# Making the first panel's neighbour masks earlier in a two-layer graph-attention kernel

## The chip, the cores and the metric

The kernel runs on one core of a Trainium2 chip. The metric is the device time of one execution in microseconds (us). A core has five engines with instruction streams of their own: TensorE (PE, matmuls), VectorE (DVE), ScalarE (ACT), GpSimd (POOL) and SyncE (SP). Here SP issues the loads and POOL the stores. Data lies in HBM, in the on-chip SBUF, and in eight PSUM banks that PE writes.

## The reference

Two attention layers over a graph of N = 2708 nodes with D = 1024 features, in float32:

```
h = relu(layernorm(x))
f, g = h @ Wf + bf, h @ Wg + bg
e = relu(f @ g.T)
x = x + softmax(where(adj > 0, e, -9e15)) @ (h @ W + bW)        # layer 0

h2 = relu(layernorm(x)) @ W1
e = leaky_relu(h2 @ a1 + (h2 @ a2).T, 0.2)
x = x + relu(softmax(where(adj > 0, e, -9e15)) @ h2)            # layer 1
```

`adj` is a 2708 x 2708 matrix of int32 zeros and ones. What the change touches is the mask made of it, in layer 0's first panel.

## The kernel before, in words

**Tiling.** The scores are made transposed, and their columns are cut into five panels of 512 to 576 (`NP = 5`). The rows run in ten pairs of 128-row tiles (`NQ = 10`); what is left over makes an eleventh unit, `LEFT`. Each product of 2 x 2 blocks is made with seven multiplications, `M1` to `M7` (Strassen's scheme).

**Stages of the beginning.** f @ g.T is h @ (Wf Wg^T) @ h.T plus bias terms, so the kernel first makes M = Wf Wg^T: a loop over `a` = 0 to 7 makes the first half rows (L607 to L624, `half_row_of_M(a, 0)`, tile M_ps), and a second loop the other half rows (L625 to L630). Meanwhile the x rows are loaded, normalized, transposed by PE (h_ps, hsT) and, for each pair, stored with their block sums in HBM (`hs_d`, and `hg_d` for the aggregation). Then `project_q(0)` (L686) multiplies M with the first panel's h (tiles qx to qz), and `scores(0)` (L1360) makes the first panel's scores pair by pair: seven products, their left sides As loaded from `hs_d`, the results in the banks sx, sy, sz. Then the next panel's projection begins (qx again), and the maximum of the scores, `acc`, is transposed by PE into mx_ps.

**Masks.** `mask_maker(p)` (L769) gives three functions for a panel. `fetch(q)` loads a pair's adjacency: four loads of adj_i (128 KB each) into a buffer of the stream pool and four of adj_t into a slot; for LEFT twice as many. `convert(q)` makes 0 or -BIG of it (nm, two DVE instructions). `turn(q, k)` transposes it in blocks of 32 x 32 (mask, two DVE instructions), and after k = 1 stores the mask in HBM (mk_d) for the second layer. In `scores` a mask is added, with a relu, by `finish`.

Before, the first masks were made beside `project_q(0)`: the hooks of its product M1 fetch pairs 0 and 1, that of M2 converts pair 0, that of M7 turns it (`first_masks`, L830). In `scores`, pair q fetches q + 2 before its first product (L1414), converts q + 1 after M5 (L1432), and turns it after M2 and M7 (L1437, L1442).

**What sets the order.** Loads go out in program order from one queue, `load` (L137), so a load that waits for its buffer holds up all behind it. Buffers come from pools in turn: 54 slots of 2304 bytes a partition, 12 stream buffers of 4 KB, 8 PSUM banks. A load's buffer is free once its last reader is through; in the scores some of the stream buffers hold rows (hsT) that a store to `hs_d` is still reading.

Work that isn't on the way of the matmuls (x rows, sums, stores) lies in a list `later`. `behind(us)` (L214) grants the list a budget of DVE time after each product, and takes items from it while the budget lasts. Each item can have a fetch, which is issued up to five items (`ahead`) before its turn. Among them are the sums of rows of `hg_d` (`sums_h`, L365; tile hr: loaded by SP, added on DVE, stored by POOL) that follow the x rows. The items' order in the list is fixed; where each falls between the products follows from these budgets, and the scheduler that builds the program may move DVE instructions that aren't held to program order.

Of the kernel before, what the change touches and what calls it, by code (L numbers as in the profile page):

```python
# [25 lines left out]
M1, M5, M6, M7, M3, M2, M4 = range(7)  # L26
# [31 lines left out]
def kernel(  # L58
# [19 lines left out]
    nc = InOrder(tc)  # L78
# [6 lines left out]
    NP = N // W  # L85
# [3 lines left out]
    width = [W + NM, W + NM, W + NY, W, W]  # L89
    base = [sum(width[:p]) for p in range(NP)]  # L90
    F = W // P
# [4 lines left out]
    start_of_tile = lambda t: base[t // F] + t % F * B32  # L96
# [40 lines left out]
    def load(o, i):  # L137
        for a, b in in_16(o, i):
            tc.keep_in_program_order(nc.sync.dma_start(a, b))

    def store(o, i):
        for a, b in in_16(o, i):
            nc.gpsimd.dma_start(a, b)  # L143
# [29 lines left out]
    mk_d = [dram.tile([P, NQ + 1, 2, width[p]], BF, name=f"mk_d{p}") for p in range(NP)]  # L173
# [7 lines left out]
    minus_half, minus_big = (consts.tile([P, 1], FP, name=f"minus{i}") for i in range(2))  # L181
# [243 lines left out]
    c0 = consts.tile([P, 1], FP, name="c0")  # L425
# [157 lines left out]
    def left_of_q(k):  # L583
# [9 lines left out]
        side_of_q(M7, k, a21)  # L593
        side_of_q(M4, k, a22)

    first_h = both("hT")
    make_pairs()
    ws = fetch_wg(0)
# [8 lines left out]
    for a in range(NC):  # L607
        for i in range(2 * a, min(2 * a + 2, NC)):
            if i + 2 < NC:
                rows_of_wf[i + 2] = load_rows(wf, i + 2, "wf")  # L610
            transposed_wf(i)
        half_row_of_M(a, 0)
        if a == NH:
            dot(c0, halves(bfb), halves(bgb))
            vb = [slot(f"vb{g}") for g in range(2)]
            for g in range(2):
                spread(vb[g][:, :W], [v[:, 4 * g + j:4 * g + j + 1] for j in range(4)])
            ws = fetch_wg(1)
        bias_of_g(a, ws)
        if a == NH + 2:  # L620
            transposed_wg(1, ws)
        behind(2.0 if a < NH else 5.0, True)
        if a == 1:
            nc.hold = ()  # L624
    for k in range(NH):  # L625
        for a in (k, k + NH):
            half_row_of_M(a, 1)
            wfT.pop(a)
            behind(5.5, True)
        left_of_q(k)  # L630
# [6 lines left out]
    for name, gs in (("pick_lo", (0, 1)), ("pick_hi", (0, 2, 3))):  # L637
        t = consts.tile([P, P], FP, name=name)
# [124 lines left out]
                   rate=1.2 if p == 0 else 1.5, room=(M1, M2, M7, M4) if p == 0 else ())  # L763
        return B


    mk_sb = {}

    def mask_maker(p):  # L769

        r0, w = base[p], width[p]
        NG, NB = P // B32, W // B32
        tail = -(-(w - W) // B32)
        raw, neg = {}, {}

        def columns(q):

            if q < LEFT:
                return [[start_of_tile(t) + P * g for g in range(NG)] for t in pairs[q]]
            return [[base[g // 2] + W + g % 2 * B32 for g in range(NG)], [base[2] + W] * NG]  # L780

        def fetch(q):
            a = stream("adj_i", (P, NB, 2, B32), I32)
            b = slot("adj_t", (P, tail, 2, B32), I32) if tail else None
            raw[q] = a, b
            c0, c1 = columns(q)

            def square_rows(t, blocks, g, k, r, j, n):
                load(t[B32 * g:B32 * (g + 1), :, k] if k is not None else
                     t[B32 * g:B32 * (g + 1)].rearrange("p b k c -> p b (k c)"),  # L790
                     adj[r:r + blocks * B32, j:j + n].rearrange("(b r) j -> r b j", r=B32))
            for t, blocks, r in ((a, NB, r0), (b, tail, r0 + W)):
                for g in range(NG if t is not None else 0):
                    if q < LEFT:
                        square_rows(t, blocks, g, None, r, c0[g], 2 * B32)
                    else:
                        for k, c in enumerate((c0, c1)):
                            square_rows(t, blocks, g, k, r, c[g], B32)

        def convert(q, by_act=False):  # L800
            a, b = raw.pop(q)
            neg[q] = []
            for t, blocks in ((a, NB), (b, tail)):
                if t is not None:
                    m = slot("nm", (P, 2, blocks, B32), BF)
                    if by_act and t is a:
                        nc.scalar.activation(m, t.rearrange("p b k c -> p k b c"), AF.Sign, bias=minus_half)
                        nc.scalar.activation(m, m, AF.Identity, bias=minus_big, scale=BIG / 2)
                    else:
                        nc.vector.tensor_scalar(m, t.rearrange("p b k c -> p k b c"), 0.0, -BIG, op0=OP.is_le, op1=OP.mult)  # L810
                    neg[q].append(m)

        def turn(q, k):
            if k == 0:
                mk_sb[p, q] = slot("mask", (P, 2, WX), BF)
            mk = mk_sb[p, q]
            m = neg[q]
            nc.vector.transpose(mk[:, k, :W].rearrange("p (s g r) -> p g s r", s=F, g=NG),
                                m[0][:, k].rearrange("p (g s) c -> p g s c", g=NG))
            if tail:  # L820
                nc.vector.transpose(mk[:, k, W:W + tail * B32].rearrange("p (b r) -> p b r", r=B32), m[1][:, k])
            if k == 1:
                neg.pop(q)
                store(mk_d[p][:, q], mk[:, :, :w])

        return fetch, convert, turn

    makers = [mask_maker(p) for p in range(NP)]

    def first_masks(p, step):  # L830
        fetch, convert, turn = makers[p]
        if step == 0:
            fetch(0)
            fetch(1)
        elif step == 1:
            convert(0)
        else:
            turn(0, 0)
            turn(0, 1)

    def load_mask(p, q, k):
        mt = slot("maskl", (P, WX), BF)
# [517 lines left out]
    def scores(p, B):  # L1360

        w = width[p]
        h = w // 2
        lo, hi = slice(0, h), slice(h, w)
        fetch, convert, turn = makers[p]
# [5 lines left out]
        acc = slot("acc")  # L1371
        S = [None] * NT
        rates = (0.6, 1.0, 0.65, 0.65, 0.65)
        lefts = {}

        def product(q, m, ps, start):
# [33 lines left out]
        for q in range(NQ):  # L1410
            n = P
            make_until(q + 2)
            rate = 1.3 if NQ - 1 not in made else rates[p]
            if q + 2 <= LEFT:  # L1414
                fetch(q + 2)
            if p in ORDERED and q in (2, 6):
                (copy_residual if q == 2 else bias_residual)(p)
            sa, sb = slot("Sa"), slot("Sb")
            S[pairs[q][0]], S[pairs[q][1]] = sa, sb
            X, Y, Z = (bank(f"s{k}") for k in "xyz")  # L1420
            m1, t = slot("sm1"), slot("st")
            product(q, M1, X, True)
            for s in (lo, hi):
                add(m1[:n, s], X[:n, :h], rb[:n, s])
            if left_over:
                left_over()
            product(q, M6, Z, True)
            add(t[:n, lo], Z[:n, :h], m1[:n, hi])
            behind(rate, True)
            product(q, M5, Y, True)  # L1430
            add(t[:n, hi], Y[:n, :h], m1[:n, hi])
            if q + 1 <= LEFT:  # L1432
                convert(q + 1, p > 0)
# [21 lines left out]
        t = stream("As", (P, 2, NH, P))  # L1455
# [245 lines left out]
    def take_softmax(p):  # L1701
        got["sm"] = softmax(p, got["S"], got["m"])

    B = project_q(0, {M1: lambda: first_masks(0, 0), M2: lambda: first_masks(0, 1), M7: lambda: first_masks(0, 2)})
    G = {}
    for p in range(NP):
        got["S"], got["acc"] = scores(p, B)
# [7 lines left out]
        if p + 1 < NP:  # L1715
            B = project_q(p + 1, hooks)
# [157 lines left out]
```

## Time and profile before

| | us |
|---|---|
| median of 3 runs | 3078.0 (3077.63 to 3078.73) |
| the profiled execution | 3082.24 |
| its span, first to last instruction | 3080.5 |
| PE busy | 3000.0 (97%) |
| DVE busy | 2046.6 (66%) |
| ACT busy | 551.7 (18%) |
| POOL busy | 505.5 (16%) |

The stages that the change touches, by the profiled execution:

| from, to (us) | stage | PE busy | DVE busy | share of the DMA engines |
|---|---|---|---|---|
| 0 to 70 | loads, first half rows of M | 58.84 of 70 | 34.76 | 0.68 |
| 70 to 157 | half rows of M, second part | 85.36 of 87 | 69.23 | 0.94 |
| 157 to 181 | projection of panel 0 begins | 24.00 of 24 | 15.16 | 0.98 |
| 181 to 224 | projection, first scores | 43.00 of 43 | 29.82 | 0.76 |
| 224 to 400 | scores of panel 0, next projection begins | 158.06 of 176 | 119.97 | 0.92 |
| 400 to 3080.5 | the rest, four panels and layer 1 | 2630.72 of 2680.5 | 1777.69 | 0.75 |

How to read it: a busy time is the union of an engine's instructions without those that only wait or issue a DMA. A row of a timeline gives start, length, engine, line of the kernel, operation, output and inputs by tile name, shape, count, and in square brackets the idle time just before it and what ended it ("<-DMA As<-hs_d": the landing of a load of As). L45 and L139 are helpers through which all DVE instructions and all loads go, so these are told apart by their tiles. PE at full clock needs 2.1 us for one product of eight matmuls on 288 columns.

### The profile page before, as it was taken

What the parts mean: (1) busy time and instruction counts of PE and PEld (TensorE: products, weight loads), DVE (VectorE), ACT (ScalarE), POOL (GpSimd) and SP (SyncE); (2) the same over time, 40 slices, a digit from 0 to 9 for tenths busy, and PEclk for the clock granted to TensorE, in tenths of its full rate; (3) what the DMA queues carried; (4) which work ended last, traced back from release to release, by engine and by line L of the source; (5) the groups of instructions that cost most, each with busy time, mean ns of one, the idle gap of its engine ahead of it and who ended that gap; (6) DMA issues with size and microseconds to landing.
All of it is one profiled execution on the core that took longest, in us unless ns stands there. A gap on an engine that the chain in (4) does not pass through costs nothing.

```text
span 3080.5 us, 41669 instructions
## 1 busy us (share of the span) xinstructions
PE 3000.0 (97%) x14630; PEld 2301.1 (75%) x14630; DVE 2046.6 (66%) x4577; ACT 551.7 (18%) x895; POOL 505.5 (16%) x786
## 2 busy tenths in 40 slices
PE   8998999899999999999999999998999999999998
PEld 4576777657877588885888886784767959879695
DVE  5776693776661586715965276867878768787853
ACT  3420020021110121101211011302222131212200
POOL 1421101310011110214102011131202010020202
PEclk9999999999999999999999999998999999999999
DMA  6988967987565786758967588679757768878786
GB/s 220 304 259 245 302 248 251 314 285 228 177 241 146 226 262 218 247 155 240 284 206 253 165 233 275 230 292 323 250 193 266 260 203 295 289 268 297 266 293 249
DMA packets 447809, 766.80 MB, mean 249 GB/s; under 512 B 175488, under 2 KB 262304, under 8 KB 447568
## 3 DMA queue, kind: packets, MB, share of 16 engines
q1 hardware_dynamic: 392624, 598.30, 60.1%
q0 software_dynamic: 54976, 165.83, 16.1%
q8 instruction: 116, 1.90, 0.2%
q14 instruction: 93, 0.76, 0.1%
HBM read 630.04 MB, written 138.11 MB: 249 GB/s over the span
## 4 chain that ended last, share of the span: by engine, by line
PE 79%; DVE 9%; DMA 5%; issue 5%; SPq 1%; ACT 1%; POOL 0%; POOLq 0%; DVEq 0%; ACTq 0%
PE sz L1385 7%; PE gz L664 6%; PE gx L664 6%; PE gy L664 6%; PE gz L1074 5%; PE pz L1274 5%; PE sx L1385 5%; PE px L1274 4%; PE sy L1385 4%; PE py L1274 4%; PE gx L1074 3%; PE gy L1074 3%; PE gv L664 3%; PE M_ps L577 3%; PE qz L664 3%
## 5 line engine op out<-in xcount | busy, mean ns | idle before, releaser
L1385 PE MATMUL sz<-B,As 128*128 128x288 f32 (+2 forms) x1200 | 292.7, 393 | 3.4 <-DVE st L45 3.3
L1385 PEld LDWEIGHTS sz<-B,As 128*128 128x128 f32 x1200 | 228.1, 191 | 53.0 <-DVE st L45 6.8
L1385 PE MATMUL sx<-B,As 128*128 128x288 f32 (+2 forms) x800 | 203.0, 397 | 13.5 <-DMA As<-hs_d 12.0
L1385 PE MATMUL sy<-B,As 128*128 128x288 f32 (+2 forms) x800 | 199.0, 392 | 0.0
L664 PE MATMUL gz<-Sa,hc 128*128 128x288 f32 (+2 forms) x800 | 190.3, 399 | 6.3 <-DMA hc<-hg_d 6.3
L1385 PEld LDWEIGHTS sx<-B,As 128*128 128x128 f32 x800 | 153.4, 192 | 47.5 <-DMA As<-hs_d 8.0
L664 PEld LDWEIGHTS gz<-Sa,hc 128*128 128x128 f32 x800 | 154.5, 194 | 40.4 <-DMA hc<-hg_d 6.7
L1385 PEld LDWEIGHTS sy<-B,As 128*128 128x128 f32 x800 | 151.7, 190 | 30.6 <-DVE st L45 0.3
L1074 PE MATMUL gz<-quarter,hc 128*128 128x128 f32 (+2 forms) x1344 | 168.8, 279 | 3.8 <-DVE gT L45 3.7
L143 POOL DMA_DIRECT2D out_dram<-x_res x180 | 89.1, 501 | 482.0 <-DVE x_res L45 473.5
L1074 PEld LDWEIGHTS gz<-quarter,hc 128*128 128x128 f32 x1344 | 160.6, 191 | 5.1 <-DVE gT L45 4.6
L1274 PE MATMUL px<-w,gT 128*128 128x512 f32 x320 | 141.2, 593 | 1.5 <-ACT pt L45 1.5
L1274 PE MATMUL py<-w,ps 128*128 128x512 f32 x320 | 142.2, 593 | 0.0
L1274 PE MATMUL pz<-w,ps 128*128 128x512 f32 x320 | 142.1, 594 | 0.0
L143 POOL DMA_DIRECT2D mk_d<-mask x55 | 36.0, 654 | 523.7 <-DVE mask L45 517.3
L1274 PEld LDWEIGHTS pz<-w,ps 128*128 128x128 f32 x320 | 60.2, 190 | 76.2 <-issue 70.5
L1274 PEld LDWEIGHTS py<-w,ps 128*128 128x128 f32 x320 | 60.5, 190 | 75.1 <-issue 72.7
L1274 PEld LDWEIGHTS px<-w,gT 128*128 128x128 f32 x320 | 60.1, 190 | 72.9 <-issue 67.1
L577 PE MATMUL M_ps<-wgT,wfT 128*128 128x512 f32 x256 | 112.5, 595 | 1.6 <-ACT hsT L45 1.6
L664 PE MATMUL gy<-T,hc 128*128 128x288 f32 (+2 forms) x480 | 111.6, 394 | 0.0
L45 ACT ACTIVATE P<-P 128x576 f32<-128x576 f32 (+2 forms) x110 | 72.0, 655 | 207.5 <-DVE P L45 207.4
L984 POOL TENSOR_TENSOR gT<-gT,rr 128x2304 f32<-128x2304 f32 (+5 forms) x12 | 44.4, 3700 | 378.0 <-DVE rr L45 172.7
(382 smaller groups left out, 5892.1 us busy)
## 6 DMA issues: line engine op xcount, KB each, us to landing
hc<-hg_d SPq DMA_DIRECT2D x175, 512.0 KB
As<-hs_d SPq DMA_DIRECT2D x150, 512.0 KB
hc<-hr_d SPq DMA_DIRECT2D x119, 512.0 KB
hc<-hs_d SPq DMA_DIRECT2D x112, 512.0 KB
w<-wt_d SPq DMA_DIRECT2D x96, 512.0 KB
w<-in_L_gnn_W_dram SPq DMA_DIRECT2D x72, 512.0 KB
md<-md_d SPq DMA_DIRECT2D x56, 512.0 KB
adj_i<-in_adj_dram SPq DMA_DIRECT2D x200, 128.0 KB
```

The lines of the kernel that those rows point to most:

```text
L45: i = f(*a, **k)
L143: nc.gpsimd.dma_start(a, b)
L577: nc.tensor.matmul(ps, wfT[a][c // NH][:, c % NH, :], wgT[b][c], start=(c == 0), stop=(c == NC - 1))
L664: nc.tensor.matmul(ps[d], left(m, k, d), right(m, k), start=(start and k == 0), stop=(k == K - 1), skip_group_check=True)
L984: nc.gpsimd.tensor_tensor(of(e, s), of(e, s), by(s, k), OP.mult)
L1074: nc.tensor.matmul(ps[:, d], lhs[:, d * P:(d + 1) * P], inner_right(m, n, k), start=(start and k == 0 and d == 0), stop=(k == NK - 1), ski ...
L1274: nc.tensor.matmul(ps, left[i][m][:, k, :], w_[k], start=(start and k == 0), stop=(k == NH - 1), skip_group_check=True)
L1385: nc.tensor.matmul(ps[:n, :h], lefts[q][:, i % 2, c, :n], B[m][c // 2][:, c % 2, :h], start=(start and c == 0), stop=(c == NH - 1), skip_g ...
```

## The change

The mask code moves up, ahead of the M stage, as it is. A new function `early_masks(q, step)` does one of three steps for a pair of panel 0. In the loop of M's first half rows, pair 0 is fetched at a = 2, converted at a = 3 and turned at a = 4; pair 1 at a = 4, 5 and 6. The hooks of `project_q(0)` now only fetch pair 2. In the scores of panel 0, `more` is 1, so that fetch, convert and turns each run one pair further ahead than before; in the other panels nothing is changed. The calls for the other panels keep `first_masks`.

```diff
+    def early_masks(q, step):
+        fetch, convert, turn = makers[0]
+        if step == 0:
+            fetch(q)
+        elif step == 1:
+            convert(q)
+        else:
+            turn(q, 0)
+            turn(q, 1)
...
         behind(2.0 if a < NH else 5.0, True)
         if a == 1:
             nc.hold = ()
+        for m in range(2):
+            if 2 <= a - 2 * m <= 4:
+                early_masks(m, a - 2 * m - 2)
...
         rates = (0.6, 1.0, 0.65, 0.65, 0.65)
+        more = int(p == 0)
...
-            if q + 2 <= LEFT:
-                fetch(q + 2)
+            if q + 2 + more <= LEFT:
+                fetch(q + 2 + more)
...
-            if q + 1 <= LEFT:
-                convert(q + 1, p > 0)
+            if q + 1 + more <= LEFT:
+                convert(q + 1 + more, p > 0)
...
-            if q + 1 <= LEFT:
-                turn(q + 1, 0)
+            if q + 1 + more <= LEFT:
+                turn(q + 1 + more, 0)
...
-            if q + 1 <= LEFT:
-                turn(q + 1, 1)
+            if q + 1 + more <= LEFT:
+                turn(q + 1 + more, 1)
...
-    B = project_q(0, {M1: lambda: first_masks(0, 0), M2: lambda: first_masks(0, 1), M7: lambda: first_masks(0, 2)})
+    B = project_q(0, {M1: lambda: early_masks(2, 0)})
```

More of the change, by code (lines that the diff above doesn't have):

```diff
@@ L594, in left_of_q, with mask_maker, columns, fetch @@
         side_of_q(M4, k, a22)
+    mk_sb = {}
+    def mask_maker(p):
+        r0, w = base[p], width[p]
+        NG, NB = P // B32, W // B32
+        tail = -(-(w - W) // B32)
+        raw, neg = {}, {}
+        def columns(q):
+            if q < LEFT:
+                return [[start_of_tile(t) + P * g for g in range(NG)] for t in pairs[q]]
+            return [[base[g // 2] + W + g % 2 * B32 for g in range(NG)], [base[2] + W] * NG]
+        def fetch(q):
+            a = stream("adj_i", (P, NB, 2, B32), I32)
+            b = slot("adj_t", (P, tail, 2, B32), I32) if tail else None
+            raw[q] = a, b
+            c0, c1 = columns(q)
+            def square_rows(t, blocks, g, k, r, j, n):
+                load(t[B32 * g:B32 * (g + 1), :, k] if k is not None else
+                     t[B32 * g:B32 * (g + 1)].rearrange("p b k c -> p b (k c)"),
+                     adj[r:r + blocks * B32, j:j + n].rearrange("(b r) j -> r b j", r=B32))
+            for t, blocks, r in ((a, NB, r0), (b, tail, r0 + W)):
+                for g in range(NG if t is not None else 0):
+                    if q < LEFT:
+                        square_rows(t, blocks, g, None, r, c0[g], 2 * B32)
+                    else:
+                        for k, c in enumerate((c0, c1)):
+                            square_rows(t, blocks, g, k, r, c[g], B32)
+        def convert(q, by_act=False):
+            a, b = raw.pop(q)
+            neg[q] = []
+            for t, blocks in ((a, NB), (b, tail)):
+                if t is not None:
+                    m = slot("nm", (P, 2, blocks, B32), BF)
+                    if by_act and t is a:
+                        nc.scalar.activation(m, t.rearrange("p b k c -> p k b c"), AF.Sign, bias=minus_half)
+                        nc.scalar.activation(m, m, AF.Identity, bias=minus_big, scale=BIG / 2)
+                    else:
+                        nc.vector.tensor_scalar(m, t.rearrange("p b k c -> p k b c"), 0.0, -BIG, op0=OP.is_le, op1=OP.mult)
+                    neg[q].append(m)
+        def turn(q, k):
+            if k == 0:
+                mk_sb[p, q] = slot("mask", (P, 2, WX), BF)
+            mk = mk_sb[p, q]
+            m = neg[q]
+            nc.vector.transpose(mk[:, k, :W].rearrange("p (s g r) -> p g s r", s=F, g=NG),
+                                m[0][:, k].rearrange("p (g s) c -> p g s c", g=NG))
+            if tail:
+                nc.vector.transpose(mk[:, k, W:W + tail * B32].rearrange("p (b r) -> p b r", r=B32), m[1][:, k])
+            if k == 1:
+                neg.pop(q)
+                store(mk_d[p][:, q], mk[:, :, :w])
+        return fetch, convert, turn
@@ new lines, with first_masks @@
+    makers = [mask_maker(p) for p in range(NP)]
+    def first_masks(p, step):
+        fetch, convert, turn = makers[p]
+        if step == 0:
+            fetch(0)
+            fetch(1)
+        elif step == 1:
+            convert(0)
+        else:
+            turn(0, 0)
+            turn(0, 1)
+    def early_masks(q, step):
+        fetch, convert, turn = makers[0]
+        if step == 0:
+            fetch(q)
+        elif step == 1:
+            convert(q)
+        else:
+            turn(q, 0)
+            turn(q, 1)
@@ L764, in project_q @@
         return B
[L767 to L839, printed above, removed]
     def load_mask(p, q, k):
```

## The prediction

> **What bounds the kernel now.** I read the page's busy times first, then the waits of TensorE (PE) in the stretch that the change touches, then the timeline of each wait.
>
> ```profile
> PE 3000.0 (97%) x14630; PEld 2301.1 (75%) x14630; DVE 2046.6 (66%) x4577; ACT 551.7 (18%) x895; POOL 505.5 (16%) x786
> ```
>
> PE is busy 3000.0 of 3080.5 us. The change adds, drops and reorders no PE instruction (in the built programs PE's order is the same), so it can only shorten or lengthen what PE idles. PE's waits from 45 us to 400 us (engine and line, what it waited for, sum, times, longest):
>
> ```profile
> PE sx L1385 <- DMA As<-hs_d: 12.0, 3, 7.5
> PE mx_ps L856 <- DVE acc L45: 5.9, 1, 5.9
> PE M_ps L577 <- ACT hsT L45: 1.6, 1, 1.6
> ```
>
> That is 19.5 us in five places. The timeline gives the places (start, length, work, idle ahead of it and its releaser), and the granted clock in three stretches says what follows a wait (the columns after the busy times are clock, DMA share, GB/s):
>
> ```profile
> 74.09 6.28 PE L577 MATMUL M_ps<-wgT,wfT 128*128 128x512 f32 x14 [1.64 <-ACT hsT L45]
> ...
> 249.34 4.21 PE L1385 MATMUL sx<-B,As 128*128 128x288 f32 x8 [7.52 <-DMA As<-hs_d]
> ...
> 285.10 3.79 PE L1385 MATMUL sx<-B,As 128*128 128x288 f32 x8 [3.90 <-DMA As<-hs_d]
> ...
> 395.11 1.33 PE L856 MATMUL mx_ps<-ident,acc 128*128 128x128 f32 x5 [5.90 <-DVE acc L45]
> ```
>
> ```profile
> 249.00:254.00 5.00, 4.66 (x10) 3.38 (x11) 0.41 (x2) 0.00 (x0) 0.00 (x0) 0.50 0.98 383
> ...
> 285.00:289.00 4.00, 3.90 (x9) 2.88 (x10) 0.08 (x1) 0.00 (x0) 0.00 (x0) 0.57 1.06 324
> ...
> 395.00:400.00 5.00, 4.89 (x17) 3.92 (x18) 5.00 (x12) 0.50 (x1) 0.72 (x1) 0.69 0.95 391
> ```
>
> A product of 8 matmuls takes 2.1 us at full clock and 4.21 and 3.79 right after the two longer waits, where the clock is 0.50 and 0.57. So the wait of 7.52 costs some 10.3 us with its slow restart (2.1 in its first product, 0.7 in the next row, 4.76 against 4.04), the one of 3.90 some 5.6, the one of 5.90 about 6.9. All five together are some 25 us, 0.8% of the time: the most that the change could win.
>
> Who sets them. At 241.8 the queue of SyncE (SP) stands from 227.3 to 239.36 before a mask's adj_i load, because that load's stream buffer still holds rows that POOL's store is writing (the chain of waits: start, length, work):
>
> ```profile
> 228.36 0.50 POOL hs_d L143
> 228.90 10.41 DMA hs_d<-hsT
> 239.36 0.33 SPq L139
> ...
> 244.55 4.75 DMA As<-hs_d
> ```
>
> The As that PE needs stands behind these eight mask loads. At 281.2 it is again a mask block ahead of an As, with one adj_t issue of 11.57 us. At 389.2 DVE has sat before a sum of hr rows that landed late:
>
> ```profile
> 389.03 0.69 DVE L45 TENSOR_TENSOR hr<-hr 128x512 f32<-128x512 f32 x1 [7.86 <-DMA hr<-hg_d]
> ```
>
> From that landing to the end of acc, which mx_ps waits for, DVE needs 395.05 - 389.03 = 6.0 us. PE had 7.9 us of other work (qx, 381.3 to 389.2) over it, so an hr that came by 383 would have cost nothing.
>
> **What the Trainium skill says.** "TensorE: Matmul & The Clock Gate", part 1 on the clock gate: after a window of some 3.4 us without work the array falls to half clock, and it needs about as long of work to come back. The rows above agree (7.52 idle, then 0.50). "DMA: Bandwidth & Descriptors", "Issuing engines are not separate DMA queues": transfers of SP and POOL share 16 engines and interleave, so a moved load is a load on whoever transfers then. From 340 to 395 us the trace has a DMA share of 1.02 at 367 GB/s[...].
>
> **The change, part by part.** One mask pair is one fetch (8 loads on SP; 16 for the last pair, LEFT), convert (0.69 + 0.23 us of DVE), two turns (0.83 us each, the price in the last pair's rows) and one store on POOL (0.54). No count changes; all of it moves.
>
> *Out of the projection, 161 to 208 us.* SP loses one block of eight loads (3.7 us of issue when unblocked: 1.84 for four adj_t, 1.95 for four adj_i). DVE loses 0.92 + 1.66 us and this stop:
>
> ```profile
> 184.43 0.69 DVE L45 TENSOR_SCALAR nm<-adj_i 128x1024 bf16<-128x1024 int32 x1 [9.03 <-DMA adj_i<-in_adj_dram]
> ```
>
> It is the most conspicuous DVE wait, and worth nothing: PE is busy 24.00 of 24.00 us from 157 to 181 and 43.00 of 43.00 from 181 to 224. Without that cover it would be up to 9 us. Gain 0.
>
> *Into the first half rows.* Pair 0's loads go behind wf's, at about 32 us; SP afterwards stands for POOL's memset from 36.44 to 56.37, so 3.7 us hide in 19.9. Pair 1's follow wg's at about 64; x of the next pairs slips by 1 to 3 us (two slots more are taken, so its loads wait for earlier dots). The x rows of pairs 2 to 5 are ready 9 to 21 us before PE turns them (108.3 and 115.2 against 129.25 for pair 3), which covers it. Convert and turns, 2 x 2.58 = 5.2 us of DVE, come at about 51, 62 to 67, 90 and 97 us; DVE is busy 11.73 of 25 us from 45 to 70, and PE 25.00 of 25. Cost 0, but for one reordering: ACT's copy of M's sixth tile comes behind the hsT copies of pairs 0 and 1, and the wait at 72.45 gets one copy (0.56) longer: +0.6.
>
> *One pair further in the scores.* SP's order in a pair is kept: the block fetched is q+3 where it was q+2, the load that waits for the hs_d store is in the same place behind the same store, and the As behind it too. I take 0 for the waits at 225.6, 241.8 and 281.2. Nothing in the trace shows how a landing of 10.41 us shifts when other loads stand before it: its bounds are the fastest transfer of the hr rows (3.6 us instead of 10.41: both waits shrink, -10) and one more adj_t stall as at 267.29 (+11.57 less PE's head start, about +8).
>
> *The end of the scores, where I expect the difference.* LEFT's 16 loads (319.2 to 332.9 us, 13.7 of issue) go in front of the preceding pair's As, and convert and turns (2.57 us) leave the last pair on DVE. SP reaches hr about 4 us sooner (350 for 354), and the shifted buffers free the later ones sooner too. But in the built program all six sums of hr rows now stand on DVE ahead of the last masking; before, four did, and the fifth's first addition. Two of them stand behind a chain: an earlier sum, its store by POOL, landing, load, landing. With this kernel's medians (6.4 us for hr's transfers from 340 to 400 us, 6.7 for the hg_d stores among them):
>
> - first sum begun and its first store given out by 358.5, landed 365.2, the fourth sum's load behind it landed 371.7, where DVE waits some 1 us with the preceding pair's additions queued behind; they end at 375.6, and PE's sx at 374.4 starts 1.2 late;
> - third sum done 370.8, its last store issued 371.7, landed 378.4, the sixth's load behind it landed 384.8;
> - from there DVE needs four additions (2.4) and 5.0 of masking: acc ends 392.2, and PE is through with qx at 390.4. PE goes on at 392.3 instead of 395.1: -2.8, and about -0.5 of slow restart.
>
> The bounds come from the same chain. With landings of 8.3 and 7.0 (as the first hr load, 354.02 to 362.06) the stall at 374.4 is 4.7 us and mx_ps starts at 396.3: +1.2. With 9.5 and 9 (near the worst, 9.7) it is 8.7 and 401: +5.9, and +9 with a restart. With 6 and 6 it is 390.6: -4.5 and -1 of restart, and no more than -6.9 is there.
>
> Sum: 0 + 0.6 + 0 - 3.3 = -2.7 us. The profiled execution took 3082.24 us, 0.14% over the median of 3078.0; I carry the difference over: **3075.3 us**. About 0.2% (6 us) is what a measurement of this kernel can tell from no change.
>
> **Rivals.** *Faster by over 0.2%:* the last wait goes wholly (-6.9) and an As wait shrinks by 2 or more, since SP has one mask block less behind it from 161 us on: about 3069. For it: hr loads would be spread over 350 to 378 instead of bunched. Against: the wait at 241.8 hangs on a store, not on SP's load. *Slower:* the chain of hr sums on DVE. It decides where loads and stores take over 8 us each: then PE's sx at 374.4 waits 5 to 9 us, and restarts at half clock: about 3086. For it: DMA at 1.02 of its share, landings there up to 9.7. Against: the medians. *Slower, another place:* a mask pair more alive takes one stream buffer of twelve and some of the 54 slots, As loads come a buffer later, and one more As wait like 281.2 appears: +6, with restart +8, about 3086 too. *No change in mechanism:* the mask loads hide where they were and PE waits as before: 3078.
>
> **How the numbers follow.** Forecast or no effect (3072 to 3084) 0.46; faster rival 0.24; the two slower ones 0.30. That gives 0.24 / 0.46 / 0.30. The range 3067 to 3089 holds the faster case but for an extra As wait gone, and the slower ones up to 11 us; for the likeliest alone it is 3072 to 3082.
>
> **What would show it.** Right: DVE's wait of 9.03 gone with no change of PE there; M's wait near 2.2; As waits near 7.5 and 3.9; mx_ps waiting 1 to 3 us for acc, and hr loads from 350. Wrong: a PE wait in the sx at 374, DVE waiting for hr twice, As waits in other pairs, or x rows late between 100 and 150 us.

## The result, and the profile after

The changed kernel is slower by about 5 us. That is under the 0.2% which the prediction called the least that can be told, but with this many executions the interval lies clear of 1: a median of 3086.13 us over 15 executions (3082.37 to 3089.63) against 3080.2 us of the kernel before beside it (15 executions). The ratio is 1.0016, 95% interval 1.0009 to 1.0023. The forecast was 2.7 us the other way. In a later series the same two kernels gave 1.0017 (1.0010 to 1.0025).

The fifteen executions of either kernel spread over 7 to 8 us, and larger sets over up to 17. The profiled one of the changed kernel is the fastest of its 15, 3082.37 us, and has the same span as the profiled one of before (3080.6 and 3080.5). So this pair of profiles can't show the 5 us; it shows where time moved. First the table of TensorE's waits up to 420 us of the changed kernel, without the two for wf and wg at the start, which are as before (microseconds in all, times, longest):

```profile
...
PE sz L1399 <- DMA As<-hs_d: 3.8, 2, 3.6
PE sz L1399 <- DVE r L45: 3.6, 1, 3.6
PE sx L1474 <- DVE sm L45: 3.2, 1, 3.2
PE sx L1399 <- DMA As<-hs_d: 2.3, 2, 1.6
PE h_ps L446 <- ACT hsT L45: 2.1, 1, 2.1
PE mx_ps L869 <- DVE acc L45: 0.4, 1, 0.4
```

L1399 is the scores' product (L1385 before), L1474 the first product of the rows left over, L869 the transposes of acc. The big wait before the masking's end (5.9 us for acc) has shrunk to 0.4, and a new one of 3.2 us stands 18 us ahead of it. In the first scores TensorE waits at more places and for less time: 6.1 us for As and 3.6 that the profile puts down to VectorE's r, 9.7 in all against 12.0 before. TensorE's rows in that stretch of time:

```profile
241.43 3.79 PE L1399 MATMUL sz<-B,As 128*128 128x288 f32 x8 [3.58 <-DVE r L45]
...
265.52 2.21 PE L1399 MATMUL sx<-B,As 128*128 128x288 f32 x8 [1.56 <-DMA As<-hs_d]
271.38 5.81 PE L1399 MATMUL sz<-B,As 128*128 128x288 f32 x16 [3.65 <-DMA As<-hs_d]
...
366.26 2.10 PE L1474 MATMUL sx<-B,As 128*128 128x288 f32 x8
...
375.55 4.21 PE L1474 MATMUL sx<-B,As 128*128 128x288 f32 x8 [3.17 <-DVE sm L45]
...
393.61 0.77 PE L869 MATMUL mx_ps<-ident,acc 128*128 128x128 f32 x5 [0.45 <-DVE acc L45]
```

The second number is the time of the group: after 3.17 us without work eight matmuls took 4.21 us, where eight of the same line took 2.10 at 366 us. This is the slow restart that the prediction took from "TensorE: Matmul & The Clock Gate", part 1 on the clock gate, of the Trainium skill, after a wait a little shorter than the some 3.4 us given there. The runs show no sharp edge at that length: eight matmuls took 3.87 us after 2.26 us without work (left_late, 238.8 us), but 2.18 after 2.25 (moved_text, 238.5 us) and 2.21 after 3.60 (after_to_scores, 243.3 us). What VectorE waited for in front of those two rows:

```profile
364.47 0.69 DVE L45 TENSOR_TENSOR hr<-hr 128x512 f32<-128x512 f32 x1 [1.93 <-DMA hr<-hg_d]
...
371.53 0.69 DVE L45 TENSOR_TENSOR hr<-hr 128x512 f32<-128x512 f32 x1 [3.11 <-DMA hr<-hg_d]
...
382.32 2.14 DVE L45 TENSOR_TENSOR hr<-hr 128x512 f32<-128x512 f32 x3 [4.28 <-DMA hg_d<-hr]
```

It is the chain that the prediction described, waits behind loads and stores of hr with the scores' own additions queued behind them. Only the end differs: by the profile the last wait is for the landing of a store itself, not for a load behind it.

Lined up by the same matmul, the changed kernel is 2.97 us ahead of before when the scores are over (399 us). That is near the forecast's 2.7, but the lead was not made where the forecast put it: at 226 us the two are level, 2.07 us came in the first scores (226 to 291 us), where nothing was forecast, and only 0.89 between 291 and 399 us, where 3.3 were.

Behind the scores the lead first grows, across a wait for a landing, in before and in the changed kernel:

```profile
549.79 6.79 PE L664 MATMUL gz<-Sa,hc 128*128 128x288 f32 x16 [6.26 <-DMA hc<-hg_d]
```

```profile
546.26 6.92 PE L751 MATMUL gz<-Sa,hc 128*128 128x288 f32 x16 [5.70 <-DMA hc<-hg_d]
```

It is 3.53 us there, 2.35 at 665 us, 1.03 at 681 us, and nothing from 1453 us on. TensorE has the same matmuls in the same order in both programs throughout, and from about 470 us on so have VectorE and ScalarE; ahead of that, six sums of hr on VectorE and some of ScalarE's work on Sa stand in other places. TensorE's waits from 640 to 1480 us, before:

```profile
PE sz L1385 <- DVE st L45: 1.9, 3, 0.8
PE sx L1385 <- DVE sm L45: 1.5, 1, 1.5
```

and after:

```profile
PE sx L1399 <- DVE sm L45: 3.3, 2, 2.6
PE sz L1399 <- DVE st L45: 3.1, 3, 1.6
```

At 665 and 1453 us VectorE is late because ScalarE is: its relu of a row, in place, has to wait until the row's store has landed. (At 681 us no store shows; VectorE is late there with dot products of its own.) ScalarE's row at 1450 us, before:

```profile
1450.41 0.81 ACT L45 ACTIVATE x_res<-x_res,rs 128x512 f32<-128x512 f32 x1 [3.56 <-DMA x_d<-x_res]
```

and after:

```profile
1450.44 0.81 ACT L45 ACTIVATE x_res<-x_res,rs 128x512 f32<-128x512 f32 x1 [4.65 <-DMA x_d<-x_res]
```

The row ends at the same time in both, 1451.2 us, though TensorE came to this place 1.06 us early in one of them. That isn't because the landing has a fixed time: the store was issued 0.71 us earlier too (1445.07 for 1445.78), but took 5.34 us to land where before's took 4.61. So this lead was lost to a slower store; why it was slower, the pair doesn't show.

### The profile page after: what moved, and what is told of

Same layout as the page of the kernel before. It is cut to its first block, busy times and chain, and to the rows that moved or that the text cites. A ratio compares the mean times of both kernels' runs of the same rounds, so it can differ in the third digit from the quotient of the medians.

```text
span 3080.6 us, 41679 instructions
## 1 busy us (share of the span) xinstructions
PE 3001.5 (97%) x14630; PEld 2301.1 (75%) x14630; DVE 2047.0 (66%) x4577; ACT 550.9 (18%) x895; POOL 504.5 (16%) x786
## 4 chain that ended last, share of the span: by engine, by line
PE 75%; DVE 11%; issue 6%; DMA 5%; POOL 1%; SPq 1%; ACT 1%; POOLq 0%; DVEq 0%; ACTq 0%
PE sz L1399 7%; PE gx L751 6%; PE gy L751 6%; PE gz L751 5%; PE gz L1087 5%; PE sx L1399 4%; PE sy L1399 4%; PE pz L1287 4%; PE px L1287 4%; PE py L1287 3%; PE gx L1087 3%; PE gy L1087 3%; PE M_ps L577 3%; PE gv L751 3%; PE qz L751 2%
## 5 line engine op out<-in xcount | busy, mean ns | idle before, releaser
L1399 PE MATMUL sz<-B,As 128*128 128x288 f32 (+2 forms) x1200 | 295.4, 396 | 12.0 <-DVE st L45 4.5
L1399 PEld LDWEIGHTS sz<-B,As 128*128 128x128 f32 x1200 | 229.1, 192 | 63.1 <-DVE st L45 8.0
L1399 PE MATMUL sx<-B,As 128*128 128x288 f32 (+2 forms) x800 | 199.4, 392 | 5.6 <-DVE sm L45 3.3
L1399 PE MATMUL sy<-B,As 128*128 128x288 f32 (+2 forms) x800 | 199.0, 392 | 0.0
L1399 PEld LDWEIGHTS sx<-B,As 128*128 128x128 f32 x800 | 151.5, 190 | 38.6 <-DVE sm L45 4.1
L1399 PEld LDWEIGHTS sy<-B,As 128*128 128x128 f32 x800 | 151.7, 190 | 30.6 <-DVE st L45 0.3
L45 ACT ACTIVATE P<-P 128x576 f32<-128x576 f32 (+2 forms) x110 | 71.9, 654 | 207.8 <-DVE P L45 207.7
```

The lines of the kernel that those rows point to most:

```text
L45: i = f(*a, **k)
L1399: nc.tensor.matmul(ps[:n, :h], lefts[q][:, i % 2, c, :n], B[m][c // 2][:, c % 2, :h], start=(start and c == 0), stop=(c == NH - 1), skip_g ...
```

## The experiments

Eighteen kernels, each timed beside the kernel before. The theories: that the sums of hr rows ahead of the last masking cost the time; that the landings of As and hs_d, which share the queues with the masks, cost it; that it is only where the buffers lie; and, later, that it arises behind the scores.

### The change again, and its parts

`after_again` is the changed kernel unaltered, for a second profile and more executions.

> The changed kernel once more, for a second profile. The first profile's time (3082.37 us) is the lowest of its 15 runs, whose median is 3086.13, so it lacks what makes the typical run slower. All theories: ratio to the kernel before 1.0016, some +5 us. Theory A (the sums of hr at the end of panel 0's scores): PE's wait for DVE's sm near 374 us is longer than the 3.17 us of the first profile, by 2 to 5 us, with a restart at half clock behind it. Theory B (As loads): the waits of sx and sz for As between 235 and 285 us sum to more than the 9.7 us of the first profile, by 4 to 6 us. Theory C (early loads): the waits before 80 us sum to 3 us more or above.

3086.11 us, ratio 1.0017 (1.0010 to 1.0025). Its profiled execution, with 3086.36 us a typical one, had 15.7 us of waits for As and 3.1 and 1.2 us at the end of the scores. That is what the theory of the As loads asked for (4 to 6 us above the first profile's 9.7), and not what the theory of the sums asked for: the wait at the end is no longer than in the first profile.

`early_only` keeps the early masks of pairs 0 and 1 but lets the scores mask one pair ahead, as before:

```
-        more = int(p == 0)
+        made_early = p == 0
...
-            if q + 1 + more <= LEFT:
-                convert(q + 1 + more, p > 0)
+            if q + 1 <= LEFT and not (made_early and q == 0):
+                convert(q + 1, p > 0)
...
-    B = project_q(0, {M1: lambda: early_masks(2, 0)})
+    B = project_q(0)
```

> Pairs 0 and 1 masked early, but the scores fetch q+2 and convert q+1 as before. Theory A and theory B, in which the cost comes from running a pair further ahead in the scores: as the kernel before, 0 +- 1.5 us. Theory C, in which the early loads cost: +4 to +6 us.

`more_only` does the opposite: no mask in M's half rows, the scores one pair further ahead; pair 1 is converted and turned, and pair 2 fetched, in the projection.

```
-        for m in range(2):
-            if 2 <= a - 2 * m <= 4:
-                early_masks(m, a - 2 * m - 2)
...
-    B = project_q(0, {M1: lambda: early_masks(2, 0)})
+    B = project_q(0, {M1: lambda: first_masks(0, 0), M2: lambda: first_masks(0, 1),
+                      M7: lambda: (first_masks(0, 2), early_masks(1, 1), early_masks(2, 0)), M4: lambda: early_masks(1, 2)})
```

> No mask in the stage of M; pairs 0 and 1 are made and pair 2 is fetched during the projection, and the scores of panel 0 run a pair further ahead as in the changed kernel. Theories A and B: +4 to +6 us against the kernel before. Theory C: 0 +- 1.5 us.

`left_late` is the changed kernel with the mask of LEFT made where it was made before. This puts the additions of hr back in their old order at the end of the scores: 18 of them ahead of the last accumulation, as in the kernel before, and not 24. (early_only and pair0_only have 18 too; more_only has 24.)

```
+        def reach(q, n):
+            j = q + n + more
+            return j if j < LEFT + 1 - more else q + n if q + n == LEFT else LEFT + 1
...
-            if q + 2 + more <= LEFT:
-                fetch(q + 2 + more)
+            if reach(q, 2) <= LEFT:
+                fetch(reach(q, 2))
```

> The changed kernel, but LEFT's mask (16 loads, convert, turns) stays where it was, in the last two pairs; all others run one pair further ahead. Theory A, if it is LEFT's move that lets all hr sums come ahead of the last masking: the wait for sm at 374 us is gone, DVE's order at the end of the scores is that of before, and the time is as before, 0 +- 1.5 us. Theory B and theory C: +4 to +6 us as in the changed kernel.

`pair0_only` makes only pair 0 early, and the scores run as before:

```
-        for m in range(2):
+        for m in range(1):
...
-        more = int(p == 0)
+        more = 0
...
-    B = project_q(0, {M1: lambda: early_masks(2, 0)})
+    B = project_q(0, {M1: lambda: early_masks(1, 0)})
```

> The smallest dose: only pair 0's mask is made early, during M's first half rows; the projection's first hook fetches pair 1, and the scores run as before. Theory D: +4 to +6 us, as the buffers shift too. Theory E with the early masks at fault: about half of the +8.6 us of the run with both pairs early, +3 to +5 us; with convert and turns of pair 1 leaving the first pair of the scores at fault: 0 +- 1.5 us, since they stay there.

| kernel | median us, executions | before beside it | ratio, 95% | in us |
|---|---|---|---|---|
| early_only | 3087.50, 13 | 3080.54 | 1.0028 (1.0019 to 1.0037) | +8.6 |
| more_only | 3085.56, 20 | 3080.54 | 1.0014 (1.0007 to 1.0022) | +4.3 |
| left_late | 3086.66, 11 | 3080.54 | 1.0016 (1.0007 to 1.0026) | +4.9 |
| pair0_only | 3085.20, 13 | 3080.36 | 1.0011 (1.0001 to 1.0021) | +3.4 |

(The last column is the ratio less one, times before.) Every part costs alone, pair0_only by an interval that only just leaves out 1, and the parts do not add up: the early masks alone cost at least as much as the whole change (8.6 and 5 us, with intervals that overlap), the other half about as much as the whole. That both halves lose fitted no single theory. In more_only, with its 24 additions, TensorE stood 5.2 us at the first product of the rows left over. TensorE's waits from 200 to 420 us, left_late:

```profile
PE sx L1404 <- DMA As<-hs_d: 10.2, 3, 4.6
PE mx_ps L869 <- DVE acc L45: 4.6, 1, 4.6
PE sz L1404 <- DMA As<-hs_d: 2.5, 2, 2.3
```

and early_only:

```profile
PE sx L1399 <- DMA As<-hs_d: 15.0, 3, 8.5
PE mx_ps L869 <- DVE acc L45: 4.0, 1, 4.0
```

In left_late the new wait before L1474's sx is gone and the old one for acc is back, and the loss is what it was. So the stall that the change put at 375 us does not by itself make the kernel slower: it only took the place of the one that ends at 395.

### Nothing moved but buffers

`moved_text` moves the mask's functions in the text alone; the program is the kernel before. `rotated` takes one slot and one stream buffer more at the start, `shuf_a` and `shuf_b` take and give back 30 and 49 in a mixed order, `swapped` declares the pools in another order. In the last four every instruction and wait is meant to be that of before, apart from memsets at the start, and the buffers lie elsewhere (in rotated, most of the slots still lie where they were).

```
+    for t in (slot("turn_s")[:, :1], stream("turn_t")[:, :1]):
+        nc.gpsimd.memset(t, 0.0)
```

```
+    held = [slot(f"held_s{i}")[:, :1] for i in range(24)] + [stream(f"held_t{i}")[:, :1] for i in range(6)]
+    for i in [26, 16, 11, 10, 23, 1, 5, 29, 7, 20, 9, 28, 17, 13, 0, 19, 22, 6, 12, 21, 14, 15, 3, 8, 2, 24, 25, 27, 18, 4]:
+        nc.gpsimd.memset(held[i], 0.0)
```

> Only the text of the mask code is moved up; the program built is the one of before, instruction for instruction, with the same buffers and waits. All theories: ratio 1.000 +- 0.0006. Its profile is a second one of the kernel before, to see which of the waits differ between executions of one program: the landings in the scores of panel 0 by up to 3 us each, PE's wait for sm at 1451 us between 1.5 and 3 us.

> The kernel before, with one more slot and one more stream buffer taken at the start (two POOL memsets of one column); every later buffer of the two pools lies one place further, and the order of the instructions is that of before. Theory D (not the masks' place but where the pools' buffers come to lie, and so what each waits for, sets the some 5 us that all four variants lost alike): +4 to +6 us. Theory E (masks moved in time cost by what they collide with): 0 +- 1.5 us.

> The kernel before, with 24 slots and 6 stream buffers taken at the start and given back in a shuffled order (30 POOL memsets of one column in the first microseconds). From then on the instructions, their order and what each waits for are those of before; only the places of the buffers in SBUF are permuted, as they are in the changed kernel and its variants. The run named rotated had left most slots where they were. Theory D (placement): +3 to +6 us, and PE's wait for DVE's sm near 1451 us is 2.0 to 3.1 us as in all six profiles with moved masks, not 1.4 to 1.5 as in the three profiles without. Theory E (masks moved in time): 0 +- 2 us, of which up to 2 are the memsets' start, and 1.4 to 1.5 us at 1451.

> The same with another permutation and more of the buffers (40 slots, 9 stream buffers, 49 memsets). Theory D: +3 to +6 us, or at least another time than the first permutation, and 2.0 to 3.1 us at 1451. Theory E: 0 to +3 us, all of it at the start, and 1.4 to 1.5 us at 1451.

> The kernel before with the two pools declared in the other order: every slot lies 48 KB higher, every stream buffer 121.5 KB lower, all in the same order; no instruction and no wait differs. Theory D, if absolute places matter: another time, -5 to +6 us. Theory D, if only the places of buffers among each other matter, and theory E: 0 +- 1.5 us.

Ratios 1.0001 (0.9992 to 1.0010), 0.9997 (0.9989 to 1.0005), 0.9997 (0.9988 to 1.0007), 1.0000 (0.9988 to 1.0011), 0.9992 (0.9981 to 1.0003). So where the buffers lie explains none of the 5 us. The sign that the expectations named, a wait of 2.0 to 3.1 us near 1453 us where the masks were moved and 1.4 to 1.5 where not, did not hold as one: it was 2.2 us in shuf_a and 1.6 in shuf_b. What these kernels leave as it was is the order in which buffers are taken, and with it the earlier use that a load's buffer has to wait for. Moving the masks changes that too, and no run tests it alone. The five also show what a profile can say: TensorE's longest wait for As in these programs, the same in order and waits, was 4.8, 8.1, 7.5, 9.2 and 8.7 us.

### Both kernels cut off

To tell whether the loss arises inside the first panel's scores or behind them, both kernels were ended at the same place, once behind these scores and once behind the aggregation of panel 1.

```
         got["S"], got["acc"] = scores(p, B)
+        if p == 0:
+            for e in range(2):
+                store(out[e * P:(e + 1) * P, :width[0]], got["acc"][:, :width[0]])
+            return
```

```
+        if p == 1:
+            return
         if p < NP - 2:
             project(0, p, G.pop(p), finish0(p), {M1: lambda p=p: first_masks(p + 1, 0),
```

> The kernel before, ended after panel 0's scores: everything behind them (softmax, aggregation, all other panels, the second layer) is left out, and two tiles of the running maximum are written out in place of the result, so that the end is the last maximum. What it runs is instruction for instruction the first 400 us of the kernel before. Alone it tests nothing; it is the measure for the next kernel. In the profiled execution of before the last maximum of the scores stands near 398 us, so 405 to 415 us with the start and the last stores, in every theory.

> The same cut of the changed kernel. Theory F (the loss of about 5 us arises where the masks were moved: waits for As and for the h sums inside the first 400 us): 3 to 6 us more than the cut of the kernel before. Theory G (the first 400 us are gained or equal, and the loss arises behind them, where the instructions are the same and only their time against the stores and loads has shifted): between 4 us less and 1 us more. The forecast on record (2.7 less) is a case of G.

> The kernel before, ended after the aggregation of panel 1 in the first layer: the other panels and the second layer are left out, and the result isn't written. Measure for the next kernel; about 1,050 us in every theory.

> The same cut of the changed kernel. Theory F: 3 to 6 us more than the cut of the kernel before, as at the first cut. Theory G with the loss at the relu of x rows behind their store (the waits of TensorE near 665 and 681 us): 1 to 4 us more than at the first cut's difference. Theory G with the loss later still (near 1453 us and in the second layer): the difference stays that of the first cut, and the full kernels' 5 us are not there yet.

Behind the scores: 378.77 and 381.11 us, means 379.1 and 380.9 over four executions each: 1.8 us more, with about 1.8 either way (95%). Behind panel 1: 1015.77 and 1015.90 us, means 1014.5 and 1016.3 over four and five executions: 1.8 us more again, but with 4.6 either way, which tells nothing. The expectation had said that the first cut is the first 400 us instruction for instruction. It is not: the sums of hr and the stores of r that only later panels read fell away with their readers, and it ended at 379 us, not at 405 to 415. So it is a test of the early masks and the As loads without the sums of hr. There the change gains nothing; its 1.8 us lie between the two theories (3 to 6, and 4 less to 1 more), and the interval just reaches 0. In the profiles of the cut kernels the waits for As in the scores are, before:

```profile
PE sz L1385 <- DMA As<-hs_d: 3.7, 2, 2.4
...
PE sx L1385 <- DMA As<-hs_d: 0.6, 2, 0.3
```

and after:

```profile
PE sx L1399 <- DMA As<-hs_d: 5.9, 2, 3.6
```

### The adj loads behind the first As loads

```
-            if q + 2 <= LEFT:
+            if p > 0 and q + 2 <= LEFT:
                 fetch(q + 2)
...
             product(q, M5, Y, True)
+            if p == 0 and q + 2 <= LEFT:
+                fetch(q + 2)
```

(in the changed kernel with `q + 2 + more`).

> The kernel before, but in panel 0's scores the eight adj loads of a pair stand on SyncE's queue behind the pair's first two As loads and not ahead of them (5 us of issuing that As stood behind at 239 to 245 us). Theory H (TensorE's waits near 242 and 281 us are the time that the As loads stand behind the adj loads): the waits for As between 225 and 295 us, 10.7 to 13.4 us in sum in the unmoved kernels, fall by 5 to 10, and the kernel is 3 to 8 us faster than before. Theory I (they are set by the landing of the hs_d stores alone, or what is gained is given back at the relu of x rows near 665 and 1453 us): within 2 us of before.

> The same edit in the changed kernel. If the change's loss of 5 us comes from the order of adj and As loads on SyncE's queue (a mask that runs a pair ahead changes which buffer an adj load has to wait for, and the As loads wait behind it): within 2 us of the kernel with the edit alone. If the loss lies elsewhere: still 3 to 7 us above it.

The kernel before became 3072.59 us with this edit, 0.9951 of before (0.9937 to 0.9964): some 15 us faster by the ratio, 12 by the means. It has only five executions, but the slowest of them (3077.52) is faster than the fastest of before's 17 beside it (3080.85), so it is the fastest version of this study and faster than both kernels. The changed kernel became 3088.51 us, 1.0003 (0.9994 to 1.0012), 16 us above it. Of the two forecasts for the pair, within 2 us of each other and 3 to 7 apart, neither came true. And the gain does not come from where it was expected. TensorE's waits from 200 to 420 us with the edit in the kernel before:

```profile
PE sx L1385 <- DMA As<-hs_d: 4.4, 1, 4.4
PE sz L1385 <- DMA As<-hs_d: 4.1, 1, 4.1
```

and in the changed kernel:

```profile
PE mx_ps L869 <- DVE acc L45: 6.5, 1, 6.5
PE sx L1399 <- DMA As<-hs_d: 5.5, 1, 5.5
PE sz L1399 <- DVE mask L45: 1.2, 1, 1.2
PE sz L1399 <- DMA As<-hs_d: 0.6, 1, 0.6
```

The waits for As fell by 3.5 us only from before's 12.0, and 2.2 us stand at a new place near 185 us. What is gone in the first is the wait for acc. Its transposes come in without a stop (row of TensorE, kernel before with the edit):

```profile
387.37 0.71 PE L856 MATMUL mx_ps<-ident,acc 128*128 128x128 f32 x5
```

There the first addition of hr begins at 369.2 us instead of 365.8, only 14 stand ahead of the last accumulation instead of 18, and none of these has to wait. In the changed kernel 21 stand there, and two of them wait, one 1.38 us and the other 7.45 (VectorE):

```profile
388.61 2.14 DVE L45 TENSOR_TENSOR hr<-hr 128x512 f32<-128x512 f32 x3 [7.45 <-DMA hr<-hg_d]
```

Lined up with before, the stretch from 291 to 399 us is 7.6 us shorter in the kernel before with the edit, and the one from 226 to 291 us, with the waits for As, 3.2 shorter. The profiled execution was one of the two slowest of the five and only 5.5 us ahead of before's in all (spans 3075.0 and 3080.5), so where the 12 to 15 us come from this profile does not show. As standing behind the adj loads explains the lesser part of what it does show.

### The sums of hr behind the last masking

A test of that place alone was meant here: the additions of hr are held to the program's order, which puts them all behind the last masking in both kernels and moves nothing on VectorE ahead of it.

```
         def first(q, two):
             (a0, a1), (b0, b1) = ((t[:, 0], t[:, 1]) for t in two)
+            held, nc.hold = nc.hold, ("vector",)
             add(b1, a1, b1)
             sub(a1, a0, a1)
+            nc.hold = held
```

(and the same around the two subtractions of `second`).

> The kernel before, with the sums of hr rows held in the program's order on VectorE, so that all of them stand behind the last masking of panel 0's scores and none ahead of it. Theory J (the h sums ahead of the last masking cost what TensorE waits there): the wait of mx_ps near 389 us (5.9 us in the page, 4.0 to 7.1 in the unmoved kernels) goes, 3 to 8 us faster. Theory K (the time is then lost at the first hc of the aggregation near 543 us, which waits for what the sums store, or later): within 2 us of before.

> The same edit in the changed kernel; VectorE's orders of the two kernels are then alike from the last masking on, and no sum of hr rows stands ahead of it in either. If the changed kernel's 5 us are the place of the h sums among the last scores (the step of the forecast that was judged the decisive one): within 2 us of the same edit in the kernel before. If they are the waits for As and the landings earlier, with the h sums having no part: still 3 to 7 us above it.

3091.95 us (21 executions), 1.0017 of before (1.0009 to 1.0024); 3093.53 us (11), 1.0024 (1.0015 to 1.0033). Both are slower than before. The wait for acc is gone in both, as expected, and a greater one stands behind it. TensorE's waits from 200 to 420 us, before with the edit:

```profile
PE qy L668 <- DMA md<-md_d: 10.6, 1, 10.6
PE sx L1389 <- DMA As<-hs_d: 7.9, 3, 4.8
PE sy L1389 <- DMA As<-hs_d: 3.7, 1, 3.7
...
```

and after with the edit:

```profile
PE qy L755 <- DMA md<-md_d: 11.0, 1, 11.0
PE sz L1403 <- DMA As<-hs_d: 9.0, 2, 5.2
PE sx L1403 <- DMA As<-hs_d: 2.9, 2, 2.4
```

The loads of hr stand on SyncE ahead of those of md (M for the next projection), and md is issued later. SyncE's rows without the edit, of the kernel before:

```profile
375.84 7.54 SPq L139 DMA_DIRECT2D hr<-hg_d  x4
387.68 20.96 SPq L139 DMA_DIRECT2D md<-md_d  x10
```

and with it, also of the kernel before (the view ends at 415 us, two loads of md short):

```profile
388.48 9.64 SPq L139 DMA_DIRECT2D hr<-hg_d  x4
398.23 13.56 SPq L139 DMA_DIRECT2D md<-md_d  x8
```

Ahead of the first of these loads of hr SyncE now waits 7.7 and 7.3 us for TensorE's sy and qx, and then, among the loads of hr, 6.4 us for a store of hr. Without the edit its waits from 376 to 388 us are for stores of hr. So only a part of the delay is shown to come from sums and stores that are later.

The difference of the two means is 1.9 us, with 1.8 either way. So with the sums of hr in one place in both kernels the change still costs, though less than 5. The pair isn't a clean comparison, though: TensorE's wait for md ends at 409.0 us in one profile and 410.2 in the other, and a wait as long as 11 us can cover differences made ahead of it.

### Twelve profiles by stage

Single profiles scatter as much as the loss, so the six of the programs whose masks were not moved (before, moved_text, rotated, shuf_a, shuf_b, swapped) were set against the six with masks moved (after, after_again, early_only, left_late, pair0_only, more_only): the time from one matmul's start to another's, the same matmuls in all, mean of the moved less mean of the others, with the standard error. The last column leaves out shuf_a, shuf_b and swapped. They come from one chip, and there the kernel before had a median of 3087.0 us, where it had 3080.4 and 3080.5 on the two chips that all others but before and after come from (for these two the chip isn't on record).

| stretch, at before's times (us) | moved less not moved (us) | without the three |
|---|---|---|
| 4.5 to 71.9, loads and M's first half rows | +0.7 ± 1.0 | +1.2 ± 1.1 |
| 71.9 to 226, M's second half rows, projection | -1.8 ± 1.5 | -0.5 ± 1.0 |
| 226 to 291, first scores: waits for As | +2.1 ± 1.4 | +1.7 ± 1.4 |
| 291 to 399, last scores, masking, sums of hr | -1.5 ± 0.6 | -2.2 ± 0.7 |
| 399 to 681, aggregation of panel 0 | +0.8 ± 0.6 | +1.2 ± 0.8 |
| 681 to 1498, with the wait at 1453 | +1.3 ± 0.6 | +1.8 ± 0.4 |
| 1498 to 3070 | -0.3 ± 0.4 | +0.3 ± 0.1 |

The sum is +1.3 ± 1.6, and +3.7 ± 2.1 without the three: so much of what the first column lacks of the 5 us may come from the choice of chips. Few of the rows are clear of chance, and the means cover kernels that differ. Taken apart they show this:

- *First scores.* after_again, early_only, left_late and pair0_only took 67.6 to 70.2 us, the six without moved masks 63.5 to 65.0. The other two were faster: the first profile of the changed kernel, the fastest of its 15 executions (62.9), and more_only (61.5). All five with masks in M's half rows have a wait for As of 0.3 to 1.6 us near 266 us, ahead of a product where none of the other seven waits.
- *End of the scores.* The three with 24 additions of hr ahead of the last accumulation (after, after_again, more_only) are 1.0 us shorter there than the six, the three with the old 18 are 1.9 shorter. So the gain in this row doesn't come from the new order of the sums. That a kernel which is late in the first scores finds its loads of hr further on, and waits less for them, is possible and not shown.
- *Behind the scores.* The store that ScalarE's relu near 1450 us waits for took 5.0 to 5.8 us in the six with moved masks and 4.5 to 5.1 in the others, and the wait of TensorE behind it was 2.0 to 3.0 us, against 1.4 to 2.2. From 399 to 681 us both groups have profiles of 282 and of 284 to 285 us.

## Why the prediction was wrong

**The projection (gain 0): right.** VectorE's wait of 9.03 us is gone, and TensorE is busy 24.00 of 24 us and 43.00 of 43 as before.

**The first half rows (+0.6): right.** The wait near 72 us was forecast at 2.2 us and was 2.08. No x row came late.

**The waits for As (0 change): a step that failed, in size.** The prediction gave them bounds of -10 and +8 and took 0. The first profile had 9.7 us in that stretch (3.6 of it behind r) against 12.0, the second one 15.7; over twelve profiles the stretch is 2.1 us longer with masks moved (standard error 1.4), in four of the six at least 2.6 us longer than in any profile without. The third rival named the mechanism, a further wait for As, and it is there near 266 us; but that wait is 0.3 to 1.6 us, and the rival asked for 6 to 8.

**The end of the scores (-3.3): the step that failed most plainly.** The stall was moved as forecast. The forecast let sx go on at 375.6 and mx_ps at 392.3; they went on at 375.55 and 393.61. VectorE waited for hr until 371.5 (forecast 371.7), and then 4.28 us for a store. But the loads of hr began at 345.7 us, not at 350, so these times hit with a chain that began earlier and took longer; and TensorE came 2 us earlier to the first of these waits than forecast, so it stood 3.17 us there and not 1.2, and restarted slowly. Before's wait for acc was dearer than the 6.9 us taken for it: without a stop the stretch from 291 to 399 us is 7.6 us shorter (before_fetch_behind, and both kernels with the sums held). But what was won at acc was paid again at sm: the stretch from 291 to 399 us is 0.89 us shorter than in before, and 1.0 us over the three profiles with the new order, which is no more than the 1.9 us of the three that kept the old one. left_late, with the old order, is as slow as the whole change. So a gain from the new order, the whole of the forecast, isn't shown at all.

**The sum: it stopped too early.** It ended at 399 us: "Sum: 0 + 0.6 + 0 - 3.3", carried over to the end of the kernel, which put every change behind the scores at nothing without a reason. That the profiled execution was 2.97 us ahead at 399 us, almost as forecast, is luck: 2.07 of it came from the waits for As. It was level behind 1453 us, after waits near 665, 681 and 1453 us, the first and the last of them behind stores of x_res rows. Over twelve profiles the stretch from 399 to 1498 us is 2.1 us longer (0.8 and 1.3), with a standard error of 0.9. The prediction never asked what TensorE waits for after 400 us, though the profile of before had those waits.

**What stays open.** The cause of the 5 us isn't shown. It is not where the buffers lie, and it is not the order of the sums alone, since left_late costs 4.9 us with the old order (2.2 to 8.0). With the sums held in both kernels the change costs 1.9 us, and in the cut kernels 1.8, both with 1.8 either way. The forecast's rival two, the sums of hr, had said 3086 us, which is the measured time; but its sign, 5 to 9 us of waiting at sx, was not there (3.2 and 3.1 us), so that it hit is luck too, as far as these runs show. The profiles point at the waits for As in the first scores and at slower stores of x_res behind them. Why either should be longer when masks are made earlier was not settled, and no run takes them away one at a time.

## What to carry to other kernels

A gain made at one place is not yet a gain at the end: after a local sum, go on down the profile, list every later wait, and ask of each whether it will still be as long. Here one wait for a landing (hc, 547 us) kept a lead of 3 us, and a later one behind a store (1450 us) lost the last of it, because the store took 0.7 us longer. Where additions for later work stand in the queue of an engine ahead of the last step that another engine waits for, look at which of them has to wait for a landing, more than at their number: 18 with one wait of 7.9 us held TensorE 5.9 us there, 24 with three shorter waits 3.2 and 0.4 us at two places, 14 without a wait not at all, and with all of them behind, TensorE stood 10.6 us for another load. A local forecast that comes out right in one profile can be right for another reason: compare it stretch by stretch. And if executions of one program differ by up to 17 us, a 5 us effect needs many executions of paired kernels on one chip; one profile of each shows mechanisms, not the difference.

## What was not expected of the hardware

One and the same order of instructions and waits gave TensorE's longest wait for As anywhere from 4.8 to 9.2 us, and executions of one program spread over 17 us (3073.6 to 3091.1 in 55 of before on one chip); the medians of before on five chips went from 3080.4 to 3088.0. All times are therefore compared with before on the same chip; the first column of the table of twelve profiles is not such a comparison, and the last only in part.
